# Column tiles in a second attention pass, a diagonal update moved from GpSimd to VectorE, a sum loaded into the gates' buffer, and mode changes in the plan

## The chip, the core and the metric

One core of one Trainium2 chip runs the whole kernel. The metric is the device time of one execution in microseconds (us). The kernel before took 1335.07 us in the median of three runs (1334.42 to 1337.16). The profiled execution has a span of 1335.1 us from its first to its last instruction.

The engines are named as in the profile. PE is TensorE, and PEld its loading of weights. DVE is VectorE, ACT is ScalarE, POOL is GpSimd, and SP is the queue that issues most transfers. Each engine takes its instructions in the order in which they were written.

## What is computed

The inputs are 32 graphs (B = 32) of 512 nodes with 128 features each, and a symmetric 0/1 adjacency of 512 x 512 for each graph. Four layers follow one another, each of the form `x = x + layer(relu(layernorm(x)))`:

```python
# layer 0: masked attention
v, q, k = relu(h @ Wv.T + bv), relu(h @ Wq.T + bq), relu(h @ Wk.T + bk)
out = softmax(q @ k.T where adj, minus infinity elsewhere) @ v
# layer 1: graph convolution with a weight made by an LSTM
dyn = conv1d(h[:, 384:, :]) + conv_b          # the last 128 nodes only
lw = lstm(dyn)                                # 128 steps, all 32 graphs at once
A = adj + eye; d = A.sum(2) ** -0.5
out = sigmoid((d[:, None] * A * d[None, :]) @ h @ lw)
# layer 2: four graph layers with skips; adjacency scaled by its rows' and columns' norms
src, dst, own = nodes @ ws + bs, nodes @ wd + bd, nodes @ wn + bn
nodes = tanh(concat(l2norm(adj, 2) @ src, own, l2norm(adj, 1).T @ dst) @ wu + bu)
# layer 3
g = adj @ (h @ W.T) + bias; out = where(g >= 0, g, prelu_a * g)
```

The LSTM is the awkward part. It needs layer 0's result for the last 128 nodes of every graph, and its 128 steps hang on one another, but nothing of layer 1's gates can start before it has ended.

## The kernel before, in words

The work is cut into three stages, and every piece of it is recorded first and ordered afterwards.

- `pass_1(b)` runs layer 0 for the last 128 nodes of graph b only, makes keys, queries and values and sends them to DRAM, and ends with the convolution that feeds the LSTM.
- `lstm()` runs the 128 steps. `pass_2(b)` runs layer 0 for the other 384 nodes of graph b at the same time, in the gaps that the LSTM leaves. For 24 of the graphs (`EARLY`) it also forms layer 1's neighbourhood sum `gT` (`sums_of_1`) and stores it in DRAM as `dgT`.
- `rest(b)` runs the gates of layer 1, layer 2 and layer 3 of graph b, and writes the output.

The order is made by `Plan.run`, a list scheduler that runs while the kernel is built. Each recorded operation has an engine (or two to choose from), a cost that was written beside it, a rank, and the tiles that it reads and writes. The scheduler puts the operation that can start first next on its engine and, among those that can start at once, the one with the lowest rank. An LSTM step's rank is below 1000 (`URGENT`): the scheduler foresees when the next urgent operation is due and doesn't place a longer one across that time. What it writes is a fixed order for each engine. The buffers are rings with a number of places each (`BUFS`); `mm` stands for the eight PSUM banks, and `kept` names the rings whose last place is reserved for operations of low rank.

These are the places that the change touches:

- LSTM step, line 1216 onwards. A step is one PE operation: four matmuls that bring the last hidden state through `W_HH` and four that bring the input of the step `MANY` = 4 places ahead through `W_IH` (line 1200). Each matmul loads 32 weight columns (one per graph) and streams 128 values, so it fills a quarter of the array's columns: the profile writes its form as `128*32`. The four of a group lie side by side in the array and fill the four quarters of the partitions of one PSUM bank. All other matmuls of the kernel use the whole array, `128*128`. The step then goes over ACT (`th`, line 1226), DVE (three operations, lines 1233 to 1235), ACT (`tcn`, line 1243) and DVE (`h` and a transpose into `seq`, lines 1247 and 1248), and the next step's matmuls read `seq`.
- Second pass, lines 1278, 1287 and 1296. Per graph one query product `f_pq` and four score products `f_s` of 384 streamed values each, and twelve products `f_po` of 129 (three output tiles times four blocks of keys), all in fp32 on the whole array. PE does an fp32 matmul in two passes, and each pass has one record in the profile.
- `diagonal`, line 1334. It adds the identity to the adjacency in place before the sum. For the 24 early graphs it runs on POOL inside the second pass, for the other eight on DVE inside `rest`.
- `aggregate`, line 1377. The sum over neighbours is eight matmuls of 512 streamed values. With `single` (early graphs) each is an operation of its own that the scheduler may part from the others; without it they come in two operations of four.
- `rest`, lines 1418 and 1434. `gT` of an early graph is loaded into a place of the ring `inv` (four places, used in order, shared with the keys and with the row of inverse norms). The gates go through tanh into another tile, `sg`, from the ring `gs` (five places).

## Time and profile before

| part of the profiled execution | us | PE busy | DVE busy | ACT busy | POOL busy |
|---|---|---|---|---|---|
| whole span | 1335.1 | 1289.0 | 1009.7 | 832.7 | 421.4 |
| first pass, 0 to 182 us | 182.0 | 172.3 | 154.4 | 108.8 | 92.6 |
| LSTM and second pass, 182 to 530 us | 348.0 | 331.3 | 288.7 | 234.0 | 124.2 |
| turn to `rest`, 530 to 620 us | 90.0 | 82.1 | 55.7 | 49.3 | 21.3 |
| `rest` in full flow, 620 to 1290 us | 670.0 | 669.0 | 485.6 | 424.7 | 177.4 |
| end, 1290 us to the last instruction | 45.1 | 34.4 | 25.3 | 15.8 | 5.8 |

How to read it: busy time is the union of an engine's instruction records. [...] records of successive matmuls overlap, so what one matmul costs is the distance between its start and the next one's start, not the length of its record. In a timeline line the first number is the start, the second the time to the end of the last of the merged records, `xN` the number of merged records, and what stands in brackets is the idle time of the engine before it with what ended it.

### The profile page before, as it was taken

The numbers are of one execution on the slowest core, as the hardware profiler recorded it, in microseconds if no ns is written. First come the engines' busy times: TensorE is split into PE (matmuls) and PEld (weight loads), VectorE is DVE, ScalarE is ACT, GpSimd is POOL, SyncE is SP. The second block draws the span as 40 slices with busy tenths as digits, with TensorE's granted clock in tenths as the row PEclk, the third lists the DMA queues.
The fourth block names the chain that finished last, engine by engine and source line by source line (L and its number), as shares of the span: only waits on it lengthen the run. The fifth ranks groups of instructions, "written<-read, shape, count | busy, mean of one in ns | idle before, by whom it ended". The sixth has DMA issues, their size and how long they took to land. (4 is left out here: it accounts for less than half of the span.)

```text
span 1335.1 us, 26488 instructions
## 1 busy us (share of the span) xinstructions
PE 1289.0 (97%) x8831; PEld 990.6 (74%) x8832; DVE 1009.7 (76%) x3388; ACT 832.7 (62%) x2093; POOL 421.4 (32%) x761
## 2 busy tenths in 40 slices
PE   7999999999999999799999999999999999999996
PEld 6888876666666666578787877778787787777774
DVE  7899878887888887756776767777776788787645
ACT  5566667776776566555666757666676666665433
POOL 4655444332243224412231322313132232232101
PEclk9999999999999999899999999999999999999998
DMA  7888888877577578963676665776777366583211
GB/s 237 278 257 278 288 261 268 261 239 232 181 232 251 165 233 211 200 177 79 134 176 157 163 161 151 157 165 152 158 162 160 89 136 134 142 161 84 48 32 35
DMA packets 302177, 236.46 MB, mean 177 GB/s; under 512 B 138320, under 2 KB 246096, under 8 KB 302032
## 3 DMA queue, kind: packets, MB, share of 16 engines
q1 hardware_dynamic: 285136, 217.90, 58.5%
q0 software_dynamic: 16896, 16.78, 8.3%
q8 instruction: 72, 1.18, 0.4%
q14 instruction: 73, 0.60, 0.1%
HBM read 140.12 MB, written 63.05 MB: 152 GB/s over the span
## 5 line engine op out<-in xcount | busy, mean ns | idle before, releaser
L1386 PE MATMUL f_pa<-f_ar,f_y 128*128 128x512 f32 x1024 | 300.9, 430 | 0.2 <-ACT f_y L1364 0.2
L1386 PEld LDWEIGHTS f_pa<-f_ar,f_y 128*128 128x128 f32 x1024 | 189.9, 189 | 73.8 <-issue 39.7
L1478 PE MATMUL f_py<-f_wf,f_n 128*128 128x128 f32 x1280 | 174.0, 275 | 0.3 <-ACT f_n L1493 0.3
L1478 PEld LDWEIGHTS f_py<-f_wf,f_n 128*128 128x128 f32 x1280 | 164.7, 191 | 8.5 <-ACT f_n L1493 0.8
L1489 PE MATMUL f_pa<-f_n,f_wf 128*128 128x512 f32 x320 | 152.8, 592 | 0.0
L1493 ACT ACTIVATE f_n<-f_pa,f_bcol 128x512 f32<-128x512 f32 x128 | 88.3, 690 | 101.7 <-PE f_pa L1489 101.3
L1330 ACT ACTIVATE f_ar<-f_a 128x512 fp32r<-128x512 f32 x224 | 138.6, 620 | 11.1 <-DMA f_a<-in_adj_dram 9.0
L1446 POOL DMA_DIRECT2D f_das<-f_ar x32 | 27.9, 872 | 346.3 <-ACT f_ar L1330 275.2
L1364 ACT CAST f_y<-f_py 128x512 fp32r<-128x512 f32 x128 | 74.9, 585 | 98.8 <-PE f_py L1478 94.8
L1296 PEld LDWEIGHTS f_po<-f_v,f_e 128*128 128x128 f32 x768 | 99.2, 190 | 23.8 <-issue 9.9
L1485 DVE TENSOR_TENSOR f_pa<-f_pa,f_inv 128x512 f32<-128x512 f32 x128 | 86.8, 692 | 34.9 <-PE f_pa L1386 34.8
L1365 DVE TENSOR_TENSOR f_y<-f_py,f_y 128x512 fp32r<-128x512 f32 x128 | 87.5, 684 | 32.9 <-ACT f_y L1364 32.3
L1296 PE MATMUL f_po<-f_v,f_e 128*128 128x129 f32 x768 | 110.2, 281 | 0.5 <-DVE f_e L1291 0.4
L1287 PE MATMUL f_s<-f_q,f_k 128*128 128x384 f32 x256 | 100.6, 502 | 0.8 <-ACT f_q L1281 0.7
L1200 PE MATMUL f_z<-f_w,f_seq 128*32 128x128 f32 x2040 | 82.2, 278 | 14.2 <-DVE f_seq L1248 8.3
L1489 PEld LDWEIGHTS f_pa<-f_n,f_wf 128*128 128x128 f32 x320 | 57.8, 189 | 45.3 <-issue 38.3
L1200 PEld LDWEIGHTS f_z<-f_w,f_seq 128*32 128x32 f32 x2040 | 48.7, 109 | 53.8 <-DVE f_seq L1248 11.7
L1451 DVE SCALAR_TENSOR_TENSOR f_junk<-f_a,f_aT 128x1024 bf16<-128x1024 f32 x64 | 78.0, 1218 | 2.4 <-DMA f_aT<-f_das 1.4
L1386 PE MATMUL f_pg<-f_ar,f_xp_d 128*128 128x512 f32 x256 | 73.8, 410 | 0.0
L1478 PE MATMUL f_py<-f_wf,f_T_c 128*128 128x128 f32 x448 | 73.0, 275 | 0.7 <-ACT f_py L929 0.7
L1290 ACT ACTIVATE f_e<-f_s 128x384 f32<-128x384 f32 x128 | 61.8, 487 | 16.6 <-PE f_s L1287 15.5
L1063 DVE COPY f_hl_d<-f_n 128x1024 uint16<-128x1024 uint16 x25 | 17.3, 693 | 66.3 <-ACT f_n L1493 66.3
(209 smaller groups left out, 2838.5 us busy)
## 6 DMA issues: line engine op xcount, KB each, us to landing
f_a<-in_adj_dram SPq DMA_DIRECT2D x56, 1024.0 KB
f_das<-f_ar POOLq DMA_DIRECT2D x32, 512.0 KB, 5.7
f_dkq<-f_kh SPq DMA_DIRECT2D x32, 448.0 KB
f_dv<-f_v SPq DMA_DIRECT2D x32, 258.0 KB
f_v<-f_dv SPq DMA_DIRECT2D x32, 258.0 KB
f_x<-in_x_dram SPq DMA_DIRECT2D x32, 256.0 KB
f_al<-in_adj_dram SPq DMA_DIRECT2D x32, 256.0 KB
f_k<-f_dkq SPq DMA_DIRECT2D x32, 256.0 KB
```

The source lines that it names most:

```text
L1200: nc.tensor.matmul(z.t[part, k, :, :], h, w[:, m : m + 4, part], start=False, stop=True, skip_group_check=True)
L1287: PE(R, t_mm(NR), lambda s=s, j=j: nc.tensor.matmul(s.t, keys.t[:, bass.ts(j, P)], q.t, start=True, stop=True), [keys, q], [s])
L1296: PE(R, t_mm(P), lambda t=t, j=j: nc.tensor.matmul(po.t[:, t, :], es[j].t[:, bass.ts(t, P)], v.t[:, j, :], start=(j == 0), stop=(j == NT - ...
L1330: ACT(rank, 0.62, lambda t=t: nc.scalar.activation(ar.t[:, t, :], a.t[:, t, :], AF.Square, accum_out=deg.t[:, t : t + 1]), [a], [(ar, t), ...
L1364: ACT(rank, t_act(N), lambda: nc.scalar.copy(parts.t[:, :, 0, :], src.t), [src], [(parts, 0)])
L1365: DVE(rank, t_dve(N), lambda: nc.vector.tensor_sub(parts.t[:, :, 1, :], src.t, f32(parts.t[:, :, 0, :])), [src, (parts, 0)], [(parts, 1)])
L1386: nc.tensor.matmul(pg.t, parts.t[:, j, k, :], ar.t[:, j, :], start=(k == 0 and j == 0), stop=(k == 1 and j == NT - 1))
L1451: nc.vector.scalar_tensor_tensor(junk, flat(a.t[:, 2 * k : 2 * k + 2, :]), 1.0, flat(aT.t[:, 2 * k : 2 * k + 2, :]), OP.mult, OP.not_equal ...
L1478: nc.tensor.matmul(py.t[:, j, :], nodes[n].t[:, bass.ts(j, P)], wf[:, W_F[i] + c, 0, :], start=False, stop=(c == nch - 1), skip_group_chec ...
L1485: before = DVE(R, t_dve(N), lambda pa=pa: nc.vector.tensor_mul(pa.t, pa.t, inv_row.t), [inv_row], [pa])
L1489: nc.tensor.matmul(pa.t, wf[:, W_F[i] + c, 1, :], nodes[n].t, start=False, stop=(c == nch - 1), skip_group_check=True)
L1493: ACT(R, 0.57, lambda pa=pa, n=n, i=i: nc.scalar.activation(n.t, pa.t, AF.Tanh, bias=bcol[:, i : i + 1]), [pa], [n])
```

## The change

It has five parts.

1. The second pass's products (`f_pq`, `f_s`, `f_po`) are split into four matmuls of 32 weight columns each, which go side by side in the array as those of the LSTM do. The values streamed and the results are the same.
2. The scheduler knows which PE operations use column tiles (`tiled`). On a change of mode it books a time before the operation (0.2 us when the next one uses the whole array, 0.1 us when it uses column tiles), and it counts that time when it chooses. The 0.1 us that every LSTM step carried for it (`T_SWITCH`) is gone, and three costs of LSTM operations are set a little differently.
3. The diagonal update runs on DVE for all graphs, and all neighbourhood sums come in two PE operations of four matmuls.
4. In `rest` an early graph's `gT` is loaded into the ring `gs` in place of `inv`. The tanh of the gates overwrites `gT`, and `sg` is gone.
5. `gs` is among the rings whose last place is kept for low ranks, the test for that also counts the reserved PSUM bank, and only operations from rank 10,000 on count as the head of the queue in it.

The diff, cut to its core:

```diff
+    SWITCH = (0.2, 0.1)
...
-        self.kept = ("mm",)
+        self.kept = ("mm", "gs",)
...
-                if len(slots[t]) < n + (t == self.banks and o.rank >= self.spared and self.left > 0):
-                    return None
-                if len(slots[t]) == n and t in self.kept and by_rank and o.rank > by_rank[-1].rank + 12:
+                spare = n + (t == self.banks and o.rank >= self.spared and self.left > 0)
+                if len(slots[t]) < spare or len(slots[t]) == spare and t in self.kept and by_rank and o.rank > by_rank[-1].rank + 12:
                     return None
...
-        by_rank = sorted((o for o in ops if o.rank >= self.URGENT), key=lambda o: -o.rank)
+        tiled = False
+        by_rank = sorted((o for o in ops if o.rank >= 10_000), key=lambda o: -o.rank)
...
                     s = max(free[e], o.ready[e], r)
+                    if e == "PE" and o.tiled != tiled and rank >= self.spared:
+                        s = max(s, free[e] + self.SWITCH[o.tiled])
...
             s, e, o = best
+            if e == "PE" and o.tiled != tiled:
+                s = max(s, free[e] + self.SWITCH[o.tiled])
...
-    T_STEP, T_SWITCH = 0.24, 0.1
+    T_STEP = 0.22
...
+    def by_columns(out, left, right, start, stop):
+        for c in range(P // TURN):
+            part = bass.ts(c, TURN)
+            nc.tensor.matmul(out[part], left[:, part], right, start=start, stop=stop)
...
-                PE(R, T_SWITCH + ahead + (T_STEP if t else 0.0), step, [], ([z] if t else []) + ([coming] if coming else []),
-                   after=last, gap=-ahead)
+                PE(R, ahead + (T_STEP if t else 0.0), step, [], ([z] if t else []) + ([coming] if coming else []),
+                   after=last, gap=-ahead, tiled=True)
...
-                DVE(R, 0.41, cell, [(th, 0), c], [u, v, cn])
+                DVE(R, 0.43, cell, [(th, 0), c], [u, v, cn])
...
-            last = [DVE(R, 0.31, out_of, [th, tcn], [h])]
+            last = [DVE(R, 0.35, out_of, [th, tcn], [h])]
...
-        PE(R, t_mm(NR), lambda: nc.tensor.matmul(pq.t, w[:, W_Q, :], hT.t, start=True, stop=True), [hT], [pq])
+        PE(R, t_mm(NR), lambda: by_columns(pq.t, w[:, W_Q, :], hT.t, True, True), [hT], [pq], tiled=True)
...
-            PE(R, t_mm(NR), lambda s=s, j=j: nc.tensor.matmul(s.t, keys.t[:, bass.ts(j, P)], q.t, start=True, stop=True),
-               [keys, q], [s])
+            PE(R, t_mm(NR), lambda s=s, j=j: by_columns(s.t, keys.t[:, bass.ts(j, P)], q.t, True, True),
+               [keys, q], [s], tiled=True)
...
-                PE(R, t_mm(P), lambda t=t, j=j: nc.tensor.matmul(
-                    po.t[:, t, :], es[j].t[:, bass.ts(t, P)], v.t[:, j, :], start=(j == 0), stop=(j == NT - 1)),
-                    [es[j], v], [po])
+                PE(R, t_mm(P), lambda t=t, j=j: by_columns(
+                    po.t[:, t, :], es[j].t[:, bass.ts(t, P)], v.t[:, j, :], j == 0, j == NT - 1),
+                    [es[j], v], [po], tiled=True)
...
-        if either:
-            POOL(rank, 1.4, on(nc.gpsimd), [], [ar])
-        else:
-            DVE(rank, t_dve(N), on(nc.vector), [], [ar])
+        DVE(rank, t_dve(N), fn, [], [ar])
...
-        diagonal(rank, ar, OP.add, b in EARLY)
-        first = aggregate(rank, xp, ar, pg, b in EARLY)
+        diagonal(rank, ar, OP.add)
+        first = aggregate(rank, xp, ar, pg)
...
-            gT, first = new("inv", (P, N), f"f_gT3_{b}"), None
+            gT, first = new("gs", (P, N), f"f_gT3_{b}"), None
...
-        sg = new("gs", (P, NT, P), f"f_sg_{b}")
         for t in range(NT):
-            ACT(R, 0.25, lambda t=t: nc.scalar.activation(sg.t[:, t, :], pl.t[:, t, :], AF.Tanh, scale=dinv.t[:, 2, t : t + 1]),
-                [pl, dinv], [(sg, t)])
-        DVE(R, 0.6, lambda: nc.vector.scalar_tensor_tensor(flat(xc.t), flat(sg.t), 0.5, flat(xc.t), OP.mult, OP.add),
-            [sg], [xc])
+            ACT(R, 0.25, lambda t=t: nc.scalar.activation(gT.t[:, bass.ts(t, P)], pl.t[:, t, :], AF.Tanh, scale=dinv.t[:, 2, t : t + 1]),
+                [pl, dinv], [(gT, t)])
+        DVE(R, 0.6, lambda: nc.vector.scalar_tensor_tensor(flat(xc.t), gT.t, 0.5, flat(xc.t), OP.mult, OP.add),
+            [gT], [xc])
```

More of the change, by code (lines that the diff above doesn't have):

```diff
@@ L517 @@
 class Op:
-    __slots__ = ("engines", "rank", "no", "deps", "cells", "waits", "ready", "end", "engine", "start", "next", "gap")
+    __slots__ = ("engines", "rank", "no", "deps", "cells", "waits", "ready", "end", "engine", "start", "next", "gap", "tiled")
 class Plan:
@@ L562, in fixed, with op @@
         return c
-    def op(self, engines, rank, reads=(), writes=(), after=(), gap=0.0):
+    def op(self, engines, rank, reads=(), writes=(), after=(), gap=0.0, tiled=False):
         o = Op()
         o.engines, o.rank, o.no, o.gap = engines, rank, len(self.ops), gap
+        o.tiled = tiled
         deps = set(after)
@@ L709, in run @@
             free[e] = o.end
+            if e == "PE":
+                tiled = o.tiled
             if o.rank < self.URGENT:
@@ L1206, in lstm @@
         z = biased(0)
-        PE(2_000, MANY * T_STEP, lambda z=z: first(z), [], [z], after=conv_ops)
+        PE(2_000, MANY * T_STEP, lambda z=z: first(z), [], [z], after=conv_ops, tiled=True)
         coming, c = z, None
@@ L1332, in squares, with diagonal, fn @@
         return ar, deg
-    def diagonal(rank, ar, op, either=False):
-        def on(engine):
-            def fn():
-                blocks = flat(ar.t).rearrange("p (k c) -> p k c", c=P)[:, :: NT + 1, :]
-                engine.tensor_tensor(blocks, f32(blocks), ident.unsqueeze(1).to_broadcast([P, NT, P]), op)
-            return fn
-        if either:
-            POOL(rank, 1.4, on(nc.gpsimd), [], [ar])
-        else:
-            DVE(rank, t_dve(N), on(nc.vector), [], [ar])
+    def diagonal(rank, ar, op):
+        def fn():
+            blocks = flat(ar.t).rearrange("p (k c) -> p k c", c=P)[:, :: NT + 1, :]
+            nc.vector.tensor_tensor(blocks, f32(blocks), ident.unsqueeze(1).to_broadcast([P, NT, P]), op)
+        DVE(rank, t_dve(N), fn, [], [ar])
     def sums_of_1(rank, b, xc, ar, rs):
@@ L1375, in relu_parts, with aggregate @@
         return parts
-    def aggregate(rank, parts, ar, pg, single=False):
-        for k, j in ((k, j) for k in range(2) for j in range(NT) if single):
-            last = PE(rank, t_r(N), lambda k=k, j=j: nc.tensor.matmul(
-                pg.t, parts.t[:, j, k, :], ar.t[:, j, :], start=(k == 0 and j == 0), stop=(k == 1 and j == NT - 1)),
-                [(parts, k), ar], [pg])
-        for k in range(0 if single else 2):
+    def aggregate(rank, parts, ar, pg):
+        for k in range(2):
             def fn(k=k):
```

## The prediction

> **What bounds the kernel now.** I began with the shares of busy time, then split the span by stage.
>
> ```profile
> PE 1289.0 (97%) x8831; PEld 990.6 (74%) x8832; DVE 1009.7 (76%) x3388; ACT 832.7 (62%) x2093; POOL 421.4 (32%) x761
> ```
>
> ```profile
> core 0: us, PE busy (x) PEld busy (x) DVE busy (x) ACT busy (x) POOL busy (x), PEclk, DMA share, GB/s
> 182.00:300.00 118.00, 112.04 (x1159) 79.78 (x1157) 99.01 (x414) 85.85 (x301) 45.24 (x72) 1.00 0.82 256
> 300.00:400.00 100.00, 94.06 (x961) 65.56 (x961) 81.65 (x335) 69.94 (x249) 34.09 (x54) 1.00 0.68 217
> 400.00:530.00 130.00, 125.15 (x1213) 84.56 (x1214) 108.07 (x472) 78.24 (x274) 44.89 (x75) 1.00 0.78 216
> 620.00:1290.00 670.00, 668.97 (x3604) 522.82 (x3603) 485.58 (x1256) 424.73 (x903) 177.44 (x272) 1.00 0.62 138
> ```
>
> PE bounds every stage. In `rest` it never stops, so only PE work counts there, and the change leaves that work alone. The stage to look at is the LSTM with the second pass: PE is busy 331.3 of 348 us, but busy with what? The PE timeline around two steps:
>
> ```profile
> 400.89 0.81 PE L1287 MATMUL f_s<-f_q,f_k 128*128 128x384 f32 x2
> 401.54 0.39 PE L1296 MATMUL f_po<-f_v,f_e 128*128 128x129 f32 x2
> 401.85 0.65 PE L1200 MATMUL f_z<-f_w,f_seq 128*32 128x128 f32 x16
> 402.42 0.91 PE L1287 MATMUL f_s<-f_q,f_k 128*128 128x384 f32 x2
> 403.17 0.39 PE L1296 MATMUL f_po<-f_v,f_e 128*128 128x129 f32 x2
> ```
>
> ```profile
> 183.18 1.30 PE L1200 MATMUL f_z<-f_w,f_seq 128*32 128x128 f32 x40
> 184.41 1.83 PE L1296 MATMUL f_po<-f_v,f_e 128*128 128x129 f32 x14
> ```
>
> Read start to start. Forty column-tile records (ten passes of four) take 1.23 us, sixteen (four passes) 0.57: six more passes cost 0.66, so one costs 0.11. A whole-array pass of 129 values costs the same 0.11 (the last `f_po`s run at 112 ns). Four column tiles therefore go side by side at the price of one full product. But 0.57 is 0.13 more than four passes; `f_po` before `f_z` takes 0.31 where two passes take 0.22; and `f_s` after `f_z` takes 0.75 where the one before took 0.65. In single records the excess is 94 ns entering the mode, 25 in its first pass, 114 leaving, and 105 in the second pass after it: 0.338 us a round trip, PE "busy" throughout.
>
> The second leak is on DVE:
>
> ```profile
> 330.07 1.26 POOL L1338 TENSOR_TENSOR f_ar<-f_ar,f_ident 128x512 fp32r<-128x512 f32 x1
> 330.13 1.26 DVE L1233 SCALAR_TENSOR_TENSOR f_cu<-f_th,f_c 128x32 f32<-128x32 f32 x1 [0.30 <-ACT f_th L1226]
> 331.31 0.23 DVE L1234 SCALAR_TENSOR_TENSOR f_cv<-f_th 128x32 f32<-128x32 f32 x1
> ```
>
> ```profile
> L1338 POOL TENSOR_TENSOR f_ar<-f_ar,f_ident x24: 1260/1276/1615, 175.5 to 465.0; 128x512 fp32r<-128x512 f32 x24
> L1338 DVE TENSOR_TENSOR f_ar<-f_ar,f_ident x16: 649/682/694, 1042.9 to 1234.0; 128x512 fp32r<-128x512 f32 x16
> L1233 DVE SCALAR_TENSOR_TENSOR f_cu<-f_th,f_c x127: 158/192/1306, 188.2 to 528.1; 128x32 f32<-128x32 f32 x127
> ```
>
> While POOL updates a diagonal, a DVE operation of the LSTM lasts 1.26 us in place of 0.19. Of the 24 updates, 22 hold up exactly one DVE operation; over its usual length that is 22.0 us in sum.
>
> [...] The trace's densest stretch, twenty `f_z` matmuls in 1.23 us less the 0.14 of mode change, ran at 55 ns each. [...]
>
> **The change part by part.** I took the fixed instruction order of both programs and priced, from each LSTM step to the next, what PE has to do: 0.109 us for a pass of four column tiles, 0.112 for one of 129, 0.3215 for 384, 0.2225 for 512 in the sums, and 0.169 per mode change.
>
> *Before:* 127 steps hold 279.4 us of passes and 254 changes (42.9 us), sum 322.3. The trace has 344.1 from first to last step, so 21.8 us are stalls; 17.0 of them lie in the 32 steps that a POOL diagonal touches, 4.8 in all others.
>
> *Column tiles.* 32 `f_pq`, 128 `f_s`, 384 `f_po` become four tiles each, at the same price per pass by the 0.11. For 384 and 129 values the trace has no tiled form. From below nothing; from above the 105 ns that a pass costs [...], on all 1088 passes: 114 us. I take nothing, since `f_z` changes weights in every pass and doesn't pay it. Issue: [...] from below nothing, which I take, after the 55 ns above.
>
> *Mode changes.* The order shows 256 before and 108 after, 86 of these between the steps (14.5 us). Passes there are 277.8 us, so PE has 292.3 us for 127 steps, 2.30 each.
>
> *Step chain.* That is near what a step needs by itself: the shortest steps of the trace took 2.16 to 2.29 us. Lifting each step of the new order to 2.2 gives 299.3 (2.1: 297.0; 2.3: 303.3). I take 2.2.
>
> *Diagonal.* DVE takes on 24 x 0.60 us (start to start in `rest`; 0.68 long) = 14.4 and loses 22.0 of stalls: 288.7 becomes 281 busy of about 304. The 17.0 us of stalls go; the 4.8 stay. POOL, SP and the transfers queued on POOL have 24 x 1.28 us less ahead of them.
>
> *Sums in fours.* Same eight matmuls, 0.89 us unbroken. Where an LSTM step falls behind one is already in the step sums, so nothing more.
>
> *`gT` in `gs`, no `sg`.* The same four tanh and one add, the same load on SP. In the order SP issues the first four loads well inside the LSTM, before many stores and loads of the second pass; each is 256 KB, the others move back by under 1 us of queue. Before, the gates waited:
>
> ```profile
> 543.77 2.05 PE L1431 MATMUL f_pl<-f_lw,f_gT 128*128 128x128 f32 x8 [3.65 <-DMA f_gT<-f_dgT]
> ```
>
> From 0 to 3.7 us may be gained, or as much lost, as four of the five `gs` places are held; I take 0.
>
> *Outside the steps.* 22 changes against 2: +3.4 us. Work that was between the steps and now follows: +1.6. Reserved-ring rules cost no instruction.
>
> Sum against the span: steps 299.3 + 4.8 = 304.1 for 344.1, -40.0; +3.4 +1.6: -35.0. From 1335.1, as good as the median of the timed runs, to **1300**. The stage's transfers, 256 x 118 + 217 x 100 + 216 x 130 in thousandths, are 80 MB; at the 275 GB/s that the first pass kept up from 25 to 182 us they need 291 us and fit.
>
> **Rivals.**
> - *The chain takes over (20%).* With PE relieved, DVE (281 of 304) and ACT queue ahead of the step. For: fewer slack places for a 0.6 us diagonal. Against: the order foresees it, and 0.19 us operations start 0.11 apart back to back, so DVE is less full than its records. Steps no shorter than 2.4 to 2.5 give 309.5 to 319.6; the upper end plus the rest: 1315.
> - *The 0.1 us gaps aren't the mode's (6%)*, but the step's semaphores. Against: the pass after the burst is late as well, with nothing to wait for. Only the 17 us of stalls go: 1318.
> - *The turn improves too (7%):* loaded `gT`s and the step at its shortest 2.1 take 6 to 10 us more: 1291 and below.
> - *Slower (4%).* [...] It decides from 35 us / 1088 passes = 32 ns a pass on; at the full 105 ns the result is 1300 + 114 = 1414. Against it: forty `f_z` records at 0.11 per four.
> - That the order doesn't do what it says is ruled out by the 108 changes.
>
> **How the numbers follow.** Forecast 63%, 1300, by itself 1291 to 1309. The range, 1287 to 1318, takes in most of the chain, semaphore and turn cases. Within 0.2% (2.7 us, about what a measurement can tell): 1%; slower 4%; faster 95%.
>
> **What would show it.** Right: from the first to the last `f_z` about 304 us; tiled `f_s` passes 0.32 apart and `f_po` 0.11; no DVE operation of 128x32 above 0.3 us; `f_sh_c` no longer up to 1243 ns; `rest` still 670 us of PE without a gap. Wrong: passes of the tiled `f_s` over 0.35 apart, PE idle in the steps waiting for `f_seq`, or a longer gap after the last step.

## The result, and the profile after

The changed kernel takes **1347.0 us** in the median of four runs (1345.35 to 1348.12), against 1334.74 us for the kernel before on the same chip: ratio 1.009, 95% interval 1.0069 to 1.0111. It is slower by 0.9%, where 1300 us was forecast. The profiled execution has a span of 1343.5 us (before: 1335.1).

The shares of busy time of the kernel after:

```profile
PE 1272.5 (95%) x12101; PEld 976.8 (73%) x12101; DVE 1003.4 (75%) x3399; ACT 835.1 (62%) x2106; POOL 382.4 (28%) x737
```

PE's busy time did fall, by 16.5 us, and the span rose by 8.4. The time saved, and more, is idle time now. Where it lies is shown by the busy time in the same stretches as before (first the stretch's ends and its length, then busy time and instructions of each engine, the granted clock, the share of the DMA engines and what they moved), kernel after:

```profile
core 0: us, PE busy (x) PEld busy (x) DVE busy (x) ACT busy (x) POOL busy (x), PEclk, DMA share, GB/s
182.00:300.00 118.00, 108.53 (x2251) 74.55 (x2243) 93.04 (x419) 86.35 (x293) 33.88 (x62) 1.00 0.78 247
300.00:400.00 100.00, 86.20 (x1574) 60.90 (x1565) 70.95 (x323) 65.36 (x237) 22.18 (x44) 0.98 0.67 211
400.00:530.00 130.00, 121.27 (x2674) 86.57 (x2673) 108.29 (x491) 88.24 (x305) 31.10 (x63) 1.00 0.69 208
530.00:620.00 90.00, 75.21 (x496) 56.42 (x497) 53.00 (x149) 50.24 (x118) 26.77 (x46) 0.92 0.86 201
620.00:1290.00 670.00, 668.24 (x3620) 523.63 (x3619) 498.40 (x1273) 419.51 (x903) 173.03 (x274) 1.00 0.61 136
```

In the three stretches of the LSTM PE is busy for 316.0 us (before 331.3), and yet the LSTM ends no sooner to speak of. The turn to `rest` has 14.8 us in which PE does nothing. `rest` itself is as full as before, and starts later.

The tiles of the LSTM and of the scores, kernel after (duration of one record, shortest/median/longest, in ns; first and last start in us):

```profile
L1218 PE MATMUL f_z<-f_w,f_seq x2040: 269/273/421, 187.7 to 526.5; 128*32 128x128 f32 x186
L847 PE MATMUL f_s<-f_q,f_k x1024: 482/486/849, 170.0 to 567.7; 128*32 128x384 f32 x171
```

The kernel issues 512 matmuls for `f_s` and the trace has 1024 records of them, two for each fp32 matmul. At 486 ns a record overlaps those of the next pass, which starts 322 ns after it in the median.

From the start of the first LSTM step to that of the last it is 338.6 us (183.2 to 527.2, or 344.1, before). The forecast had 304. From the last step to the end it is 817.1 us, where it was 807.9. The first step starts 4.6 us later (187.7 against 183.2), which no run here explains. Beside that, the loss has two parts: LSTM steps that hardly became shorter although PE had 30 us less to do in them, and a turn that became longer.

What PE waits for in the LSTM, kernel after (who waited, in which line, for whom: us in sum, times, the longest):

```profile
PE f_z L1218 <- DVE f_seq L1266: 11.3, 14, 3.7
PE f_po L847 <- issue: 6.7, 4, 2.9
PE f_z L1218 <- issue: 3.7, 2, 2.9
PE f_s L847 <- issue: 3.2, 3, 1.5
ACT f_x L1053 <- DMA f_dx<-f_x: 9.9, 5, 3.7
DVE f_x L1050 <- DMA f_dx<-f_x: 9.5, 8, 3.2
ACT f_ar L1348 <- DMA f_a<-in_adj_dram: 7.9, 4, 2.5
```

Three things are new beside the kernel before. PE has "issue" waits (idle time in which the profile shows nothing that PE waits for; 13.6 us in these rows, and the kernel before has no such wait of PE). ACT and DVE, which carry the LSTM's step, wait for transfers for 27.3 us (before: 5.8 in the same three rows). And PE waits for `f_seq` for 11.3 us, 3.0 more than before.

### The profile page after: what moved, and what is told of

Read it like the earlier page. It is cut to its first block, busy times and chain, and to the rows that moved or that the text cites. A ratio compares the mean times of both kernels' runs of the same rounds, so it can differ in the third digit from the quotient of the medians.

```text
span 1343.5 us, 33035 instructions
## 1 busy us (share of the span) xinstructions
PE 1272.5 (95%) x12101; PEld 976.8 (73%) x12101; DVE 1003.4 (75%) x3399; ACT 835.1 (62%) x2106; POOL 382.4 (28%) x737
## 5 line engine op out<-in xcount | busy, mean ns | idle before, releaser
L1395 PEld LDWEIGHTS f_pa<-f_ar,f_y 128*128 128x128 f32 x1024 | 189.1, 188 | 76.3 <-issue 38.0
L847 PE MATMUL f_po<-f_v,f_e 128*32 128x129 f32 x3072 | 107.9, 275 | 8.3 <-issue 6.7
L847 PE MATMUL f_s<-f_q,f_k 128*32 128x384 f32 x1024 | 102.4, 490 | 7.6 <-issue 3.2
L1454 POOL DMA_DIRECT2D f_das<-f_ar x32 | 27.9, 873 | 286.3 <-ACT f_ar L1348 228.8
L847 PEld LDWEIGHTS f_po<-f_v,f_e 128*32 128x32 f32 x3072 | 91.1, 111 | 25.1 <-issue 17.1
L1218 PE MATMUL f_z<-f_w,f_seq 128*32 128x128 f32 x2040 | 85.0, 277 | 17.7 <-DVE f_seq L1266 11.3
L1218 PEld LDWEIGHTS f_z<-f_w,f_seq 128*32 128x32 f32 x2040 | 55.2, 109 | 53.5 <-DVE f_seq L1266 13.9
L1395 PE MATMUL f_pg<-f_ar,f_xp_c 128*128 128x512 f32 x256 | 73.0, 416 | 0.3 <-ACT f_xp_c L1385 0.3
```

What stands on the lines that cost most here:

```text
L847: nc.tensor.matmul(out[part], left[:, part], right, start=start, stop=stop)
L1218: nc.tensor.matmul(z.t[part, k, :, :], h, w[:, m : m + 4, part], start=False, stop=True, skip_group_check=True)
L1395: nc.tensor.matmul(pg.t, parts.t[:, j, k, :], ar.t[:, j, :], start=(k == 0 and j == 0), stop=(k == 1 and j == NT - 1))
```

## One step of the LSTM, hand-over by hand-over

The forecast added up PE's work. The runs below need another view: the six hand-overs of a step. The engines keep to the written order: in the trace of before PE's 8831 records, DVE's 3388 and ACT's 2093 and SP's 829 issues of transfers come in the order in which the kernel wrote them, and after so do those of DVE (3399), ACT (2106) and SP (829). So a hand-over waits for what its engine has ahead of it. Timeline of the kernel after, two steps in which little stands in the way:

```profile
406.70 0.62 PE L1218 MATMUL f_z<-f_w,f_seq 128*32 128x128 f32 x16
407.17 0.25 ACT L1244 ACTIVATE f_th<-f_z 128x96 f32<-128x96 f32 x1
407.45 0.19 DVE L1251 SCALAR_TENSOR_TENSOR f_cu<-f_th,f_c 128x32 f32<-128x32 f32 x1 [1.04 <-ACT f_th L1244]
408.07 0.23 ACT L1261 ACTIVATE f_tcn<-f_c 128x32 f32<-128x32 f32 x1
408.33 0.19 DVE L1265 SCALAR_TENSOR_TENSOR f_h<-f_th,f_tcn 128x32 f32<-128x32 f32 x1 [0.35 <-ACT f_tcn L1261]
408.63 0.21 DVE L1266 STREAM_TRANSPOSE f_seq<-f_h 128x32 f32<-128x32 f32 x1
408.99 0.65 PE L1218 MATMUL f_z<-f_w,f_seq 128*32 128x128 f32 x16
```

From `f_z` to `f_th` 0.47 us, to `f_cu` 0.28, to `f_tcn` 0.62, to `f_h` 0.26, to `f_seq` 0.30, to the next `f_z` 0.36: 2.29 us, and PE's queue can delay only the last one (and the first, where something comes between a step's own matmuls). With the shortest that the last one usually gets (0.27) and these others the step takes 2.20 us, and that is what a saving on PE can reach. (The shortest single step of any run took 2.07.) The table adds each hand-over over the steps of a run, from start to start in the trace (126 of the 127 steps; the very first is left out). It is read from one execution of each run. Timed executions of one and the same kernel lie 2.5 to 11.5 us apart here, so a us or two in the steps means nothing. The runs are told of further down.

| us in sum | f_z to f_th | f_th to f_cu | f_cu to f_tcn | f_tcn to f_h | f_h to f_seq | f_seq to f_z |
|---|---|---|---|---|---|---|
| before | 66.7 | 49.4 | 85.6 | 43.9 | 28.3 | 65.9 |
| `b_tiles` | 70.8 | 50.6 | 84.2 | 43.2 | 29.4 | 61.1 |
| `b_diag` | 66.0 | 45.9 | 78.8 | 43.5 | 27.8 | 67.1 |
| `b_both` | 69.5 | 51.1 | 76.3 | 43.0 | 27.7 | 61.9 |
| `d_po1` | 70.0 | 52.5 | 77.3 | 43.6 | 28.0 | 56.4 |
| `d_po1_nomask_exp` | 67.9 | 50.0 | 78.4 | 41.0 | 28.1 | 54.7 |
| `a_whole` | 67.9 | 37.2 | 83.2 | 43.3 | 27.9 | 76.8 |
| after | 77.2 | 39.6 | 84.8 | 42.3 | 27.9 | 63.8 |
| `a_no_adj` | 66.6 | 41.9 | 78.2 | 43.3 | 27.9 | 54.7 |

## The experiments

Two theories stood at the start. One: PE sets the pace of the steps as forecast, and something new holds PE up, either the supply of its instructions or the transfers of the new order. The other: a step's chain over DVE and ACT sets the pace, so that work taken from PE there turns into waiting. Each run's steps are the distance from its first to its last `f_z` start.

### One part alone, in the order of before

The order of the kernel before is kept here: only what an operation issues is exchanged, and the scheduler's costs aren't touched. `b_tiles` has the column tiles alone, `b_diag` the diagonal on DVE alone, `b_both` both.

```diff
 # b_tiles: by_columns as in the change, for f_pq, f_s and f_po
-            PE(R, t_mm(NR), lambda s=s, j=j: nc.tensor.matmul(s.t, keys.t[:, bass.ts(j, P)], q.t, start=True, stop=True),
+            PE(R, t_mm(NR), lambda s=s, j=j: by_columns(s.t, keys.t[:, bass.ts(j, P)], q.t, True, True),
...
 # b_diag
-            POOL(rank, 1.4, on(nc.gpsimd), [], [ar])
+            POOL(rank, 1.4, on(nc.vector), [], [ar])
```

> The kernel before in its own instruction order, with nothing changed but that f_pq, f_s and f_po are each issued as four column tiles. The order then has 140 mode changes for 256. Theory A (PE's supply of instructions: the split adds 6,528 PE records, [...] and PE runs dry): waits of PE put down to issue appear, over 0.5 us each and 5 to 15 us in sum, and eat much of 116 x 0.169 = 19.6 us; about 1322 to 1332 us. Theory B (the new order is what is bad: it leaves transfers too little time, and DVE and ACT stand before an LSTM operation waiting for a transfer): this order has the old slack, no issue waits over 2 us in sum, about 1315 us. Theory C (a column tile costs more than a quarter of a pass): f_s passes over 0.35 apart and f_po over 0.13; slower than before.

> The kernel before in its own instruction order, with nothing changed but that the 24 diagonal updates of the second pass are issued on DVE, at the place in the order where POOL had them. All theories: no 128x32 DVE operation over 0.4 us, and 17 us of stalls in the steps gone, less what a 0.6 us update in front of an LSTM operation costs (24 x 0.3 = 7 us): 1318 to 1326 us. If the gain is under 5 us, the update's place in DVE's order holds up the chain as much as POOL did, and that part of the prediction is wrong.

> The kernel before in its own instruction order, with the column tiles and the diagonal on DVE together, nothing else. Passes 279.4 us, 140 mode changes (116 fewer, 19.6 us). Theory A with the reading that the mode changes were slack in which other delays hid: alone the tiles gave nothing since 21 steps waited about 1 us each behind a POOL diagonal; with those gone the tiles pay: 1326 less 19.6 plus 4 to 8 us of issue waits, 1308 to 1316 us. Theory D (with PE relieved some other resource, transfers or the DVE and ACT order, holds the stage at 330 to 345 us whatever PE does): no faster than the diagonal alone, 1322 to 1330 us.

| run | time, us | ratio (95% interval) | steps, us | mode changes between the steps, us of PE | PE idle in the steps, us |
|---|---|---|---|---|---|
| before | 1334.7 | | 344.1 | 42.9 | 15.8 |
| `b_tiles` | 1336.9 | 1.000 (0.9985 to 1.0015) | 343.3 | 19.6 | 28.2 |
| `b_diag` | 1326.2 | 0.993 (0.9905 to 0.9949) | 332.9 | 42.9 | 6.3 |
| `b_both` | 1327.7 | 0.994 (0.992 to 0.996) | 333.0 | 19.6 | 19.4 |

Each ratio is to the kernel before on the same chip, where it took 1334.6 to 1336.6 us in the median; two times from different chips are best compared by their ratios. The mode changes are counted in each order and priced at 0.169 us each, the forecast's price.

The diagonal does what was forecast of it. Of `b_diag`, the tiles that POOL had held up:

```profile
L1233 DVE SCALAR_TENSOR_TENSOR f_cu<-f_th,f_c x127: 157/192/218, 189.0 to 518.1; 128x32 f32<-128x32 f32 x127
L1043 DVE SCALAR_TENSOR_TENSOR f_sh_c<-f_ln,f_rs x24: 119/155/164, 186.1 to 465.5; 128x4 f32<-128x4 f32 x24
```

The longest `f_cu` is 218 ns, where it was 1306. The steps are 11.2 us shorter, and the time is 10.4 us under that of the kernel before on its chip (1336.6).

The tiles do nothing for the time, twice: with them PE has 23.3 us less to do between the steps, and the steps stay within 0.8 us of what they were. In the table of hand-overs the last column falls by 4.8 us (`b_tiles`) and 5.2 us (`b_diag` to `b_both`). It would have fallen by 9 to 11 us, but for seven and eight steps that now wait over half a microsecond longer than usual there (6.2 and 8.2 us over the usual in sum; three such steps without the tiles, 1.7 and 2.0 us). In each run the longest of them is a wait of PE for a transfer (`f_w`, 1.8 and 2.1 us), and one is an issue wait. The other columns take back 4.3 and 5.6 us, so that nothing is left. The issue waits are two in each run, 3.8 and 3.0 us in sum, fewer than theory A's 5 to 15; the time of `b_tiles` is none of the three theories'. `b_both` came as theory D had it.

### How much of PE's work matters at all

`d_po1` takes 58 us off PE with no mode and no tile in question. On the order of `b_diag` it leaves nine of the twelve `f_po` products of each graph in the second pass out.

```diff
-                PE(R, t_mm(P), lambda t=t, j=j: nc.tensor.matmul(
-                    po.t[:, t, :], es[j].t[:, bass.ts(t, P)], v.t[:, j, :], start=(j == 0), stop=(j == NT - 1)),
+                PE(R, t_mm(P), lambda t=t, j=j: j == t and nc.tensor.matmul(
+                    po.t[:, t, :], es[j].t[:, bass.ts(t, P)], v.t[:, j, :], start=True, stop=True),
```

> The kernel before in its own order with the diagonal on DVE, whole-array second pass, but of the twelve f_po products of each graph only the three are left in that multiply a query tile with its own block of keys; the attention's output is therefore another. PE has 32 x 9 x 0.2235 = 64 us less to do (58 of them between the steps), DVE, ACT and the transfers the same, and no instruction is added. If PE sets the pace of the steps (my prediction), they fall from 332.9 to 298 us, the sum with every step lifted to 2.2 us. Theory D (the step's own chain, through DVE and ACT with other work in front of it, takes about 2.5 us whatever PE has to do): 320 us or more (lifted to 2.5: 322).

Measured: 1323.3 us, ratio 0.991 (0.9895 to 0.9933). The steps take 331.6 us, 1.3 less than in `b_diag`. The same stretches in `b_diag`:

```profile
182.00:300.00 118.00, 116.16 (x1203) 82.71 (x1202) 99.14 (x436) 88.77 (x311) 34.38 (x63) 1.00 0.83 269
300.00:400.00 100.00, 97.49 (x1000) 68.85 (x1001) 82.40 (x367) 74.29 (x262) 27.56 (x52) 1.00 0.71 229
```

and in `d_po1`:

```profile
182.00:300.00 118.00, 101.02 (x1063) 65.11 (x1066) 100.73 (x448) 89.87 (x321) 35.56 (x64) 1.00 0.85 273
300.00:400.00 100.00, 85.03 (x817) 52.93 (x813) 79.92 (x357) 72.15 (x253) 26.88 (x50) 0.93 0.68 222
```

PE falls from 98% busy to 86 and 85%, and DVE and ACT do about as much in the same time as before. Of the 58 us taken away 45 became idle time of PE (6.3 to 51.4 us). The granted clock fell as well: its mean over the steps is 0.97 here and 1.00 in `b_diag`, by estimate 10 us of PE's work at full speed (0.03 of 331.6). That is most of what isn't idle time, and far less than what was taken away. PE's work doesn't set the pace of the steps; theory D had 320 us or more.

### DVE, then DVE and PE, then all three

If not PE, is it DVE's load, at 83% the fullest of the others? `both_nomask` is `b_both` without the 128 products of the second pass with the mask (some 60 us of DVE). `d_po1_nomask` leaves the same products out of `d_po1`. `d_po1_nomask_exp` besides forms only those blocks of the exponentials on ACT that the three products left read.

```diff
 # both_nomask, d_po1_nomask, d_po1_nomask_exp
-            DVE(R, t_dve(NR), lambda e=e, j=j: nc.vector.tensor_mul(e.t, e.t, rows_of(j)), [(mask, j)], [e])
+            DVE(R, t_dve(NR), lambda: None, [(mask, j)], [e])
...
 # d_po1_nomask_exp
-            ACT(R, t_act(NR), lambda s=s, e=e: nc.scalar.activation(e.t, s.t, AF.Exp), [s], [e])
+            ACT(R, t_act(NR), lambda s=s, e=e, j=j: j < 3 and nc.scalar.activation(
+                e.t[:, bass.ts(j, P)], s.t[:, bass.ts(j, P)], AF.Exp), [s], [e])
```

> The kernel before in its own order with column tiles and the diagonal on DVE, but without the 128 mask products of the second pass on DVE (128 x 0.47 = 60 us of DVE, the attention is therefore unmasked). PE, ACT and the transfers have the same work. Theory D with DVE as what stands in front of the chain: the steps fall from 333 towards PE's own sum of 299 to 305, to 318 us or less. If they stay over 327, DVE isn't what lengthens the chain, and ACT, transfers or the blocks of instructions are.

> Leaves out, on the order of before with the diagonal on VectorE: nine of the twelve products f_po of each graph in the second pass (58 us of PE in the LSTM steps) and all 128 mask products there (about 60 us of DVE). Step stretch (first to last f_z) of the same order with nothing left out 332.9 us, with the PE products alone left out 331.6. If PE and DVE hold the step together, so that taking from one alone can't show: at most 305 us. If it is the step's own chain with ACT's queue and the waits for transfers: 318 to 328, what the mask products alone gave (6.5 us) or a little more, and PE idle of over 40 us stays.

> As the last, and of the second pass's exponentials on ACT only the blocks that the products left over read (a third of three of four; the fourth is left out): some 40 us of ACT less in the steps. If ACT's queue in front of the gates is what holds the step: 25 us or more below the run without this edit. If what holds the step is the chain's own five operations and its hand-overs, and the waits for transfers: less than 10 us below it, and f_z still waits for f_seq in most steps; the step stays over 2.3 us in the mean although PE, DVE and ACT were each given 40 to 60 us.

| run, on the order of before | taken away beside its forerunner | time, us | steps, us | PE idle in the steps, us |
|---|---|---|---|---|
| `b_diag` | | 1326.2 | 332.9 | 6.3 |
| `d_po1` | 58 us of PE | 1323.3 | 331.6 | 51.4 |
| `d_po1_nomask` | and 60 us of DVE | 1315.0 | 326.2 | 47.6 |
| `d_po1_nomask_exp` | and 40 us of ACT | 1312.5 | 323.8 | 49.1 |
| `b_both` | | 1327.7 | 333.0 | 19.4 |
| `both_nomask` | 60 us of DVE | 1325.3 | 326.5 | 14.0 |

What PE waits for in `d_po1_nomask_exp`, in the stretch of the LSTM:

```profile
PE f_z L1200 <- DVE f_seq L1248: 26.2, 28, 4.4
```

The taking away is nearly without effect: with 40 to 60 us less for each of the three engines that a step runs over, it is 9.1 us of 332.9. A step still takes 2.55 us in the mean. So the load of none of the three engines is the bound. In the table of hand-overs five of the six columns of this run lie within 4.1 us of `b_diag`'s, and only the last, the one that PE's queue can delay, falls, by 12.4 us. Most of a step is the bare length of the chain: 2.20 us by the steps shown above, 279 us for 127 of them. The rest is what a hand-over meets by chance in a queue (a whole instruction of the second pass, or one that waits for a transfer). The expectation that PE would wait for `f_seq` in most steps was too high: the row counts 28. And 326.5 us in `both_nomask` is 6.5 less than in `b_both`, a tenth of what was taken off DVE and between the two cases of its expectation. In time the two aren't told apart (ratios of 0.994 and 0.993). What isn't separated by these runs is how much of the rest each queue and each transfer adds. The transfers are a rival that was left untested in this order: ACT's and DVE's waits for `f_dx` and `f_a` in the LSTM grow as the engines are relieved, from 4.0 us in `b_diag` to 10.8, 12.2 and 16.7 us in the three runs of the `d_po1` kind. No run leaves transfers out of the order of before.

### The new order

Are PE's issue waits a price of the tiles, and what does the new order cost by itself? `a_whole` has the order of the kernel after and issues whole-array products in it. `a_no_adj` is the kernel after without the adjacency loads of the 24 early graphs in the second pass (the squares read ones in their place): 24 MB of transfers less in the same order, with the same records on PE.

```diff
 # a_whole: by_columns
-        for c in range(P // TURN):
-            part = bass.ts(c, TURN)
-            nc.tensor.matmul(out[part], left[:, part], right, start=start, stop=stop)
+        nc.tensor.matmul(out, left, right, start=start, stop=stop)
...
 # a_no_adj
-            DMA(R, 1024, lambda: nc.sync.dma_start(a.t, adj[b].rearrange("(t p) j -> p t j", p=P)), [], [a])
-            ar, deg = squares(R, b, a, "2")
+            DMA(R, 1024, lambda: None, [], [a])
+            ar, deg = squares(R, b, a, "2", True)
```

> The changed kernel in its own instruction order, with nothing changed but that f_pq, f_s and f_po are issued as one whole-array matmul each. 256 mode changes return for 108: up to 74 x 0.338 = 25 us more PE work, 4,896 to 6,528 PE records fewer. Theory A: the issue waits (13 us of PE) go to under 2 us; 1347 + 25 - 13 = about 1359, less where waits hide the mode changes: 1350 to 1359. Theory B: issue waits may go, but DVE's and ACT's waits for f_dx and f_a (25 us) stay; about 1355 to 1370. If it is faster than 1340, column tiles cost more than they save.

> The changed kernel in its own instruction order, but the second pass of the 24 early graphs doesn't load the adjacency (24 x 1 MB less of some 80 MB in that stage); ACT squares a constant tile of ones in its place, so the masks and layer 1's sums are other values. All other work is the same. Theory A: [...] issue waits under 3 us. Theory B: waits for f_dx go as well. If both hold, the steps come down to my sum of 299 to 304 us from 338.6, and the time to 1305 to 1315 us. If the order of the LSTM's own chain is at fault, neither matters: steps over 325 us.

| run | time, us | ratio (95% interval) | steps, us | PE's work between the steps, us | single issue waits of PE over 0.3 us, in sum |
|---|---|---|---|---|---|
| after | 1347.0 | 1.009 (1.0069 to 1.0111) | 338.6 | 292.3 | 12.9 |
| `a_whole` | 1346.1 | 1.008 (1.0043 to 1.0111) | 339.7 | 320.7 | 0 |
| `a_no_adj` | 1324.8 | 0.992 (0.9887 to 0.9949) | 315.6 | 292.3 | 2.6 |

`a_whole` and the kernel after take the same time, although PE has 28.4 us more to do between the steps in `a_whole`. That is the third pair of this kind, but more than PE's work differs in it: ACT and DVE wait for `f_dx` and `f_a` for 12.7 us in `a_whole` and for 27.3 in the kernel after, and PE's issue waits are 0 and 12.9. The hand-overs show where. From `a_whole` to after the last column falls by 13.0 us, the gain from the tiles; but the first rises by 9.3 us, the second by 2.4 and the third by 1.6. In the last column of the kernel after six steps are 13.4 us over the usual in sum, and five of these, with 12.1 us, are issue waits of PE (the tiles save PE 28.4). In the first column eight steps are 11.9 us over the usual in sum; in six of these the ACT timeline shows ACT waiting for a transfer in front of `f_th`. This fits a step that comes to that hand-over sooner and waits there. Both expectations of `a_whole` (1350 us and more) were too high, and that of `a_no_adj` (1305 to 1315 us) too low.

In the new order the transfers hold up the steps: `a_no_adj` shortens them by 23.0 us and the time by 22. The waits of ACT and DVE for `f_dx` and `f_a` fall by 17.5 us (27.3 to 9.8, in the rows shown above) and the issue waits by 10.3; what each is worth alone isn't separated. Nor is it shown that the order of before would gain less from the same edit: from `b_both` to the kernel after the steps differ by 5.6 us only. A timeline of the kernel after shows one such wait:

```profile
293.26 0.34 DVE L1050 TENSOR_SCALAR f_x<-f_x,f_ln,f_rs 128x128 f32<-128x128 f32 x1 [3.20 <-DMA f_dx<-f_x]
293.32 0.88 ACT L1053 ACTIVATE f_x<-f_x,f_sh_c,f_rs 128x128 f32<-128x128 f32 x2 [3.73 <-DMA f_dx<-f_x]
294.84 0.65 PE L1218 MATMUL f_z<-f_w,f_seq 128*32 128x128 f32 x16 [3.70 <-DVE f_seq L1266]
```

The layer norm overwrites `f_x` in place and must wait until the store `f_dx` has read it. That store was issued at 284.88 and the adjacency (1 MB) had been put in the queues at 282.83, ahead of it. DVE stands for 3.20 us and ACT for 3.73, an LSTM step is queued behind both, and PE gets `f_seq` 3.70 us late. In `a_no_adj` the waits of ACT and DVE for `f_dx` are 5.5 us, in the kernel after 19.4. One difference between the two orders is seen in SP's own waits, kernel after:

```profile
SPq L1291 <- DMA f_dgT<-f_x: 59.9, 17, 7.4
```

and kernel before:

```profile
SPq L1273 <- DMA f_dgT<-f_x: 22.8, 11, 5.0
```

SP stands 59.9 us, in 17 waits, in front of a load whose place the store of `gT` still occupies, and what is behind it in SP's queue stands as well: in the longest, 7.4 us, SP issues nothing from 285.3 to 292.76. That this is what brings the waits of ACT and DVE was not tested.

The issue waits come from the tiles, since `a_whole` has none; but the traffic has a part in them, since `a_no_adj` has the same records and 2.6 us in the steps (and one wait of 3.1 us after the last step). A timeline of the kernel after shows one of the five long ones:

```profile
278.31 0.60 DVE L1320 SCALAR_TENSOR_TENSOR f_x<-f_po,f_rinv,f_x 128x128 f32<-128x128 f32 x2
281.00 0.52 PE L847 MATMUL f_po<-f_v,f_e 128*32 128x129 f32 x10 [2.88 <-issue]
281.89 0.25 ACT L1244 ACTIVATE f_th<-f_z 128x96 f32<-128x96 f32 x1 [3.52 <-PE f_z L1218]
```

PE stands for 2.88 us in which the profile shows nothing that it waits for, and ACT waits for `f_z` behind it. In the page's part on the DMA queues a row for queue 8 is named "instruction" (packets, MB, share). After:

```profile
q8 instruction: 98, 1.61, 0.5%
```

and before, where PE has no issue wait:

```profile
q8 instruction: 72, 1.18, 0.4%
```

These are 26 packets of 16,384 bytes more, in a program with 6547 instructions more (33035 and 26488): by estimate some 252 instructions to a packet. Counted over all records of PE and of its weight loading (24588), the five long waits lie multiples of 256 records apart, within two, and each ended 2.36 to 2.45 us after a packet of queue 8 had begun. From these figures it is the author's estimate that PE waits for its own instructions there; the profile names nothing that PE waits for.

### The turn

At the turn to `rest`, ACT and PE of the kernel after:

```profile
535.92 1.92 ACT L1444 ACTIVATE f_gT<-f_pl,f_dinv 128x128 f32<-128x128 f32 x7 [1.45 <-PE f_pl L1440]
544.04 0.63 ACT L1348 ACTIVATE f_ar<-f_a 128x512 fp32r<-128x512 f32 x1 [6.20 <-DMA f_a<-in_adj_dram]
546.50 0.35 ACT L1444 ACTIVATE f_gT<-f_pl,f_dinv 128x128 f32<-128x128 f32 x1
548.30 1.09 PE L852 MATMUL f_xt_c<-f_ident,f_xn_c 128*128 128x128 f32 x4 [8.17 <-ACT f_xn_c L1053]
```

Seven of the gates' tanh are done, and the eighth stands in ACT's queue behind squares of an adjacency whose load SP issued at 535.13 only. What the eighth finishes is needed for PE's next matmuls, and PE stands for 8.17 us. The wait for `f_gT` that was shown of before (3.65 us) is gone. `a_turn` is the kernel after, with the adjacency of the first six graphs of `rest` not loaded there (the squares read ones, and the comparison of the adjacency with its transpose compares the transpose with itself).

```diff
-        DMA(R, 1024, lambda: nc.sync.dma_start(a.t, adj[b].rearrange("(t p) j -> p t j", p=P)), [], [a])
+        unread = b < 6
+        DMA(R, 1024, lambda: unread or nc.sync.dma_start(a.t, adj[b].rearrange("(t p) j -> p t j", p=P)), [], [a])
```

> The changed kernel in its own order, but rest doesn't load the adjacency of the first six graphs; ACT squares ones, and the check for symmetry compares the turned copy with itself, so the output of these graphs is another. At the turn ACT waited 6.2 us for such a load ahead of the gates' tanh, and PE stood still for 8.2. If that load's late issue is the cause, PE's idle time in the 60 us after the last step falls from 15 to under 8 us, and the time from 1347 to about 1338 to 1341. If the turn is long for the chain from the gates to the first products, it stays over 12 us and the time over 1343.

Measured: 1344.7 us, ratio 1.007 (1.005 to 1.0084). PE's idle time in the 60 us after the last step goes from 15.2 to 10.1 us, and from the last step to the end it takes 814.2 us in place of 817.1. This load is part of the turn's loss: PE's wait of 8.2 us for `f_xn_c` is 1.0 us there. The result lies between the two cases of the expectation, and the two time ratios overlap, so the gain in time isn't clear of noise. What keeps the rest of the loss isn't shown; PE's longest wait there is now 2.8 us for ACT's `f_hT_c`.

### The scheduler's view

`e1_diag` makes the diagonal's move known to the scheduler and lets it plan anew: one operation per early graph on another engine at another cost, and nothing else. `e6_gap4` is the kernel after with 4 us booked for a transfer in place of 2.

```diff
 # e1_diag
-        if either:
-            POOL(rank, 1.4, on(nc.gpsimd), [], [ar])
-        else:
-            DVE(rank, t_dve(N), on(nc.vector), [], [ar])
+        DVE(rank, t_dve(N), on(nc.vector), [], [ar])
...
 # e6_gap4
-        return plan.op({"SP": (max(0.45, t_dma(kb)), fn)}, rank, r, w, gap=2.0, **k)
+        return plan.op({"SP": (max(0.45, t_dma(kb)), fn)}, rank, r, w, gap=4.0, **k)
```

> The kernel before with the diagonal on DVE for all graphs and known to the scheduler as a DVE operation of 0.6 us, so that the whole order is made anew; whole-array second pass, POOL untouched otherwise. If the gain of the diagonal alone (1326 us) was limited by its unplanned place, planning gives 3 to 6 us more: 1320 to 1324. If a new order as such brings waits for transfers (theory B), it loses them again: 1328 to 1340 us, with waits for f_dx and f_a over 8 us on DVE and ACT.

> The changed kernel, with nothing but the time that the scheduler books from a transfer's issue to its landing set to 4 us in place of 2 us; the order is made anew. Theory B (the order relies on transfers landing sooner than they do): DVE's and ACT's waits for transfers fall from 28 us to under 10 us, and the time to 1325 to 1337 us; issue waits stay near 13 us. Theory A alone: no gain beyond 5 us, 1342 to 1350 us.

| run | time, us | ratio (95% interval) | steps, us | last step to the end, us | PE idle after the turn, us |
|---|---|---|---|---|---|
| `b_diag` (same work as `e1_diag`) | 1326.2 | 0.993 (0.9905 to 0.9949) | 332.9 | 805.4 | 10.8 |
| `e1_diag` | 1416.6 | 1.062 (1.0595 to 1.064) | 337.4 | 893.0 | 57.0 |
| after | 1347.0 | 1.009 (1.0069 to 1.0111) | 338.6 | 817.1 | 12.3 |
| `e6_gap4` | 1359.4 | 1.019 (1.0169 to 1.0212) | 333.8 | 832.0 | 14.9 |

The busy times of `e1_diag` in `rest` show that it isn't the LSTM:

```profile
530.00:620.00 90.00, 62.18 (x259) 42.03 (x258) 43.82 (x136) 35.49 (x84) 23.07 (x36) 0.85 0.51 126
620.00:1290.00 670.00, 635.34 (x3338) 490.48 (x3338) 445.80 (x1136) 404.81 (x873) 157.89 (x257) 0.98 0.58 133
```

PE is idle for 28 us of the turn and 35 of the 670. The same instructions in two orders are 90 us apart: one changed cost led the scheduler to another order, down to the end of the kernel. Both cases of its expectation (1340 us at most) were far off. In `e6_gap4` the transfers' waits do as theory B said: in the three rows ACT and DVE wait for 7.5 us in place of 27.3. The steps are only 4.8 us shorter with it, at issue waits of 13.2 us, and the time is longer, since the new order loses 14.9 us after the last step. Theory B's time (1325 to 1337 us) was wrong. `b_both` and the kernel after hold the comparison that the change is about: the same tiles and the same diagonal, once in the order of before and once in the new one (with the new places of `gT`). That is 1327.7 against 1347.0 us.

## Why the prediction was wrong

**"PE bounds every stage"**, the first reading, failed for the LSTM's steps, and with it the sum that rested on it. The busy shares there were 95, 94 and 96 hundredths (112.04 of 118, 94.06 of 100, 125.15 of 130), but a busy PE in that stretch was working ahead with what it would have done later, and what it saved turned into waiting. Four pairs show it: 23.3 us off PE (before to `b_tiles`) shorten the steps by 0.8 us, 23.3 (`b_diag` to `b_both`) by nothing, 28.4 (`a_whole` to after) by 1.1, and 58 (`b_diag` to `d_po1`) by 1.3. The last is the clean one, as it adds no instruction and has no issue wait in the steps; the tiles of the other three bring issue waits of 3.0 to 12.9 us with them. By the lines of before weight loading was busy 230 of 348 us, 66%, and DVE 83%; 60 us less on DVE gave 6.5 us.

**"Step chain"** is the step of the sum that failed. It took 2.2 us as a floor under each step, from the shortest steps of the trace, and added PE's own time wherever that was longer: 299.3 us. The floor is right as the bare chain: 2.20 us by hand-overs. As a length of the usual step it is wrong. The mean of a run in which PE, DVE and ACT were each relieved of 40 to 60 us is still 2.55 us. Five hand-overs hardly depend on PE, each finds something in DVE's or ACT's queue now and then, and the waits add along the chain where the sum took the larger of two figures. The rival that the chain takes over had the mechanism, at 2.4 to 2.5 us a step. The step was 2.67 (338.6 over 127): the rival reckoned with DVE's and ACT's load and left out the waits for transfers (27.3 us) and the issue waits (12.9 us).

**"Mode changes" and "Column tiles"**: the prices were right. PE in the kernel after:

```profile
414.20 1.50 PE L847 MATMUL f_s<-f_q,f_k 128*32 128x384 f32 x16
415.49 0.65 PE L847 MATMUL f_po<-f_v,f_e 128*32 128x129 f32 x16
```

Sixteen records of `f_s`, four passes, take 1.29 us from start to start. Record by record, in the median, tiled `f_s` passes lie 0.322 us apart, tiled `f_po` passes 0.110, and `f_po` after `f_z` follows at 0.109 with nothing for a change. So PE's sum between the steps, 292.3 us by order and prices, stands. It just wasn't what the time hung on: the steps were to exceed that sum by 11.8 us (304.1 less 292.3) and exceed it by 46.3. Most of the forecast's signs of being right came true with it (the distances of the passes, DVE's operations at most 228 ns, 668.2 of 670 us in `rest`): they tested the prices, and only the 304 us tested the path.

**"Issue"** was taken as nothing, by the 55 ns of a matmul in the densest stretch of before. The tiled passes kept that rate: four tiles of `f_po` went at 0.110 us a pass, 55 ns again for each matmul with its two records. But 12.9 us of issue waits were not foreseen. They lie on the chain: the last hand-over of the kernel after holds 12.1 us of them. That `a_whole` has none and takes as long doesn't make them cheap, since PE has 28.4 us more to do there; what removing them alone gives wasn't measured.

**"Diagonal"** was right in this: no operation of the LSTM on DVE is held up any more (the longest takes 228 ns, where it was 1306). Of the 17.0 us of stalls 11.2 came out of the steps in the order of before, and 10.4 us out of the time. In the new order its gain can't be told apart from the order's own waits.

**The order.** "Outside the steps" had +5.0 us and "*gT* in *gs*" 0, and the rules for the rings "cost no instruction". That was the other large miss: a rule of a scheduler costs no instruction, and it moves all of them. From `b_both` to after the spans differ by 14.8 us: 1.6 before the first step, 5.6 in the steps, 7.5 after the last one. Of the last, 6.5 us are PE's idle time in the turn (15.2 against 8.7). The DMA share of the turn rose from 0.64 to 0.86, and the forecast had weighed transfers only by their sum over the LSTM ("they fit"), not by who waits for a single one. The medians are 19.3 us apart, so some 4 us more aren't placed by these traces. Which of the scheduler's edits (the mode changes booked, the reserved places, the changed costs) is to blame stays open too; they weren't run one by one.

**The forecast of a slower result** needed a dear column tile (32 ns or more over the price on each of 1088 passes, 4%), which didn't come: the passes went at 0.322 and 0.110 us. The slower result came by the new order, for which no case was made.

Of the runs that leave no work out `b_diag` is the fastest, at 1326.2 us: the diagonal on DVE in the order of before, 0.7% under the kernel before and some 1.5% under the kernel after. With the tiles besides (`b_both`) it isn't faster.

## What to carry to other kernels

Where a serial chain runs through a stage, list its hand-overs from start to start and ask for each which queue can delay it, before a busy engine is called the bound; a busy engine may be filling the chain's gaps. The shortest step of a chain is the floor of a step and not its length. If a change alters what a scheduler knows, keep the old order and exchange only what is issued: that prices the edit, and what is left is the price of the order.

## What was not expected of the hardware

- PE can stand under load with nothing that the profile shows it waits for: five issue waits of 1.3 to 2.9 us, multiples of 256 records apart within two, in a program with four times the records per product in the second pass and a DMA share of about 0.7; none in `a_whole`, with whole products, and 2.6 us of waits in the steps with 24 MB of transfers less.
- Four column tiles of 32 go at the price of one whole-array pass for 129 and 384 streamed fp32 values as well (0.110 and 0.322 us; whole in the kernel before 0.112 and 0.323).
- Taking 58 us of matmuls from a PE that is 98% busy (116.16 of 118 us in `b_diag`) changed the LSTM's steps by 1.3 us (332.9 to 331.6).
